# Segment attention with a batch norm: the order of the closing sums, and the split of the output stage over VectorE, TensorE and the queues

## Chip, cores and metric

The kernel runs on one core of one Trainium2 chip. The metric is the device time of one execution in microseconds (us). The kernel before takes 324.0 us, the median of three runs (323.58 to 324.59).

## The reference

16384 rows of 256 floats carry a segment number from 0 to 7 each. The numbers are random and not sorted, yet the start of every segment is looked up with `searchsorted`. Each segment attends over its own rows, the result goes through a matrix, a batch norm over all rows follows, and a relu of it is added to the input.

```python
q, k, v = feat @ Wq, feat @ Wk, feat @ Wv
starts = jnp.searchsorted(bids, jnp.arange(8))
pos = jnp.arange(N) - starts[bids]
qp, kp, vp = pad(q), pad(k), pad(v)            # zeros(8, 3072, .).at[bids, pos].set(.)
attn = softmax(where(mask, qp @ kp.T, -1e9))   # per segment
r = (attn @ vp)[bids, pos]
t = r @ Wt
tn = (t - t.mean(0)) / sqrt(t.var(0) + 1e-5) * gamma + beta
return feat + relu(tn)
```

Because the numbers are not sorted, `pos` can be negative or 3072 and more. A position past an end reads the segment's edge row; a negative one wraps round, and if two rows meet in one place only one of them is stored ("losers" read the other's result). So there are three kinds of output rows: rows that own a place (at most 768 a segment), losers, and rows that read an edge row of some segment.

## The kernel before

`fast_path` writes one instruction stream per engine by hand; a small planner (`Program.op`, `Program.run`) puts in the semaphore waits that the operands call for. Within an engine the order is the order of the code. The helpers record every operation, so many instructions share a line: L803 is every matmul, L813 every activation, L818 and L819 copies on ScalarE and VectorE, L822 `tensor_tensor`, L831 `tensor_scalar`, L842 `scalar_tensor_tensor`, L855 the reciprocal, L878 a gather, L894 a scatter (`put`), L886 a scatter inside a branch (`put_now`).

**Attention.** A loop over the eight segments (`for e in range(NB)`) gathers a segment's rows in tiles of 128 (`xs`), projects, scores, and attends; `attend` leaves the sums and the row weights in PSUM, `scale` writes the rows `tk`, and these are stored in DRAM (`t_rows`). In between, `moments` adds each finished row tile and its square into `acc` on VectorE, and `square` makes the squares on ScalarE.

**The closing sums.** In the last segment, a gather on GpSimd's queue fetches the edge rows into `ecat` from `t_rows`. Edge rows that belong to the last segment are picked out by matmuls into `b_e` and added (L1786), and the square of the sum goes into the other half of `ecat` (L1787). Both lines stand ahead of the last row tile (`u == 3`) in the streams of VectorE and ScalarE. After the loop, two matmuls of 512 columns finish the column sums: `we` times `ecat` (L1876), then `ones` times `acc` (L1877). From `sums` VectorE makes mean, variance, `scale` and `shift`, then the edge rows' outputs `y3` in two bf16 parts (L1878 to L1922).

**The output stage.** The rows of the output are written twice. First every row of 16 *groups* of 1024 rows (1 MB each) is written as input plus edge output; then the owner rows and the losers are scattered over them. A group `k` of eight row tiles is four *pairs* of 512 columns. A one-hot matmul (`hot`, 16 matmuls a group, bf16) puts each row's edge output into PSUM. The list `PAIRS[k]` says how many of the four pairs TensorE adds up itself: `open_group` runs the input through an identity matmul into the same bank, and ScalarE copies the sum back. VectorE adds the other pairs to PSUM (`f` L822).

```python
PAIRS = [1, 1, 0, 0, *(2,) * 7, 1, 1, 0, 1, 0]
```

SyncE's queue then issues the group's `store` (L1960), waits in `finish(stores[k - 1])` (L1953) until the store of the group before has landed and counts it in the semaphore `done`, and may issue a load. There are `NF` = 10 buffers for the 16 groups: groups 0 to 9 are loaded before the stage, groups 10 to 15 within it, one behind the store of each group from 3 to 8 (L1988, L1989). `finish` and the load stand behind the store in one queue, so both wait for what the store waits for.

The order of the groups is a table made from the data, such that groups a segment's rows lie in come early. `upto` holds, for each segment, how many groups have to be done before its rows may be scattered. With the reference's inputs it is 3, 5, 5, 7, 7, 7, 11, 11 for the segments, 11 for the losers. Their row counts are 436, 511, 542, 726, 701, 698, 431 and 468, and there are 199 losers.

`normal(m, 4)` makes the output of a segment's first four row tiles on VectorE, three instructions of 1024 columns; `normal_more` does a fifth and a sixth tile (256 columns) in a branch that is taken only if the segment has them. Before, segment `e` follows group `e + 3`, and the losers (`tl`, three tiles, 768 columns) follow group 11.

On GpSimd, each segment's scatters wait for `done` and for these rows. There are four scatters a segment, seven more in branches that these inputs take (one for segment 2, two each for segments 3, 4 and 5), and `LT` = 3 for the losers, in all 42. Each addresses 128 rows; an index past the end is skipped by the transfer. The scatters count in a semaphore `loose`, and the engine waits at the end until it has the number that the register `rows` holds.

Of the kernel before, what the change touches and what calls it, by code (L numbers as in the profile page):

```python
# [11 lines left out]
I32 = mybir.dt.int32  # L12
BF16 = mybir.dt.bfloat16
F16 = mybir.dt.float16
AF = mybir.ActivationFunctionType
ALU = mybir.AluOpType
# [4 lines left out]
P = 128  # L21
NB = 8
# [6 lines left out]
FT = 6  # L29
FW = FT * P  # L30
LT = 3
# [870 lines left out]
def fast_path(nc, feat, bids, wq, wk, wv, wt, gamma, beta, out, bad):  # L902
    N, D = feat.shape
# [5 lines left out]
    NG = J // GT  # L909
    NL = NB + 1  # L910
    TT = NB * FT
# [14 lines left out]
    def new(name, shape, dtype=F32):  # L926
        nonlocal end
        size = mybir.dt.size(dtype)
        for d in shape[1:]:
            size *= d  # L930
        plan.append((name, shape, dtype, end))
        h = at(name, shape, dtype, end)
        end += size + -size % 32
        return h
# [53 lines left out]
    eidx, ridl, idxo = new("eidx", [P, 1], I32), new("ridl", [P, LT], I32), new("idxo", [P, LT], I32)  # L988
    eps_t = new("eps_t", [P, 1])
    armf, arm = new("armf", [1, NB]), new("arm", [1, NB], I32)  # L990
    upto, order = new("upto", [1, NB + 2], I32), new("order", [1, NG], I32)
    gb = new("gb", [P, 2, 32])
    gt_, bt_ = gb[:, 0, 0:NB], gb[:, 1, 0:NB]
    mq, ss8 = new("mq", [P, 2, NB]), new("ss8", [P, 2, NB])
# [75 lines left out]
    def load(eng, key, ap, hi, lo=0):  # L1070
        def emit(e):
            regs[key] = e.value_load(ap, min_val=lo, max_val=hi)

        pg.op(eng, emit, [ap], [], bare=True)
# [642 lines left out]
    def load_group(k):  # L1717
        f = fb[k % NF]

        def emit(e):  # L1720
            rows = feat[ds(regs[("order", k)] * GR, GR), :]
            return e.dma_start(f[:], rows.rearrange("(p i) d -> p i d", p=P))

        pg.op("SP", emit, [], [f[:]], dma=True)

    for e in range(NB):
        last = e == NB - 1
        n = e + 1
        if e == 1:
            one, two, three_ = edges()  # L1730
            sides = [*side_count(0, below[:]), *side_count(1, above[:])]
            fills = fill_rows()
            work.extend([fills[0], *one, fills[1], two, *sides, fills[2], *three_, lambda: own_of(NB - 1)])
        if not last:
            size_of(n)
        pg.region_of((e,) if last else (e, n))
        if e == 0:
            xt_rest(0)
            values(0, 1)
            project(0, 1)  # L1740
            values(0, 2)
            scores(0, 0, range(4, 6))
            own_of(2)
            zero_fill(2)
        if last:
            for u in (0, 1, 4, 5, 2, 3):
                step(e, u)
                if u == 0:
                    scores(e, 1, range(4))
                    late[2]()  # L1750
                    pg.gather(ecat[:, 0, :], t_rows[0 : (NB - 1) * FW, :], eidx[:], (NB - 1) * FW)
                    for g in range(FIRST, EARLY):
                        load_group(g)
                if u == 1:
                    scores(e, 1, range(4, 6))
                    late[4]()
                if u == 4:
                    late[3]()
                if u == 0:
                    lag[:0] = [(NB, t) for t in range(LT)]  # L1760
                if u == 5:
                    first = square(e, 1)
                    for g in range(EARLY, MID):
                        load_group(g)
                if u == 1:
                    pg.act(row_sum[:], ones[:], AF.Identity, scale=reads_r[:, e * FT + 1 : e * FT + 2])
                if u == 3:
                    any_ = hot[0 : 2 * NB, 0:2, :, :].rearrange("p k u x -> p (k u x)")
                    pg.mm(sums[:], none[0 : 2 * NB, :], any_, start=True, stop=False)
                    by_row(row_sum, first[0], first[2])  # L1770
                if u == 3:
                    while lag or squared:
                        if lag and len(squared) < 2:
                            squared.append(square(*lag.pop(0)))
                        else:
                            moments()
                else:
                    past(e)
                if u == 2:
                    b_e = ps_s[0]  # L1780
                    for u_ in (0, 4, 5, 1):
                        pg.mm(
                            b_e[:, 0:D], sel[:, u_, :], tk[:, e * FT + u_, :], start=(u_ == 0), stop=(u_ == 1),
                            pred=over4(e, u_),
                        )
                    pg.tt(ecat[:, 0, :], ecat[:, 0, :], b_e[:, 0:D], ALU.add)  # L1786
                    pg.act(ecat[:, 1, :], ecat[:, 0, :], AF.Square)  # L1787
        else:
            busy = e + 2 < NB
            step(e, 0, lambda: (xt_main(n, 0), xt_main(n, 1)))  # L1790
            if 0 < e < NB - 3:
                prefix(e + 2, e + 3)
                sizes(e + 2)
            if 0 < e and busy:
                list_ahead(e + 2)
            scores(e, 1, range(4))
            past(e)
            slot()
            if e == NB - 2:
                load_group(0)  # L1800
            step(e, 1)
            xt_rest(n)
            if e == 0:
                prefix(e + 2, e + 3)
                sizes(e + 2)
                list_ahead(e + 2)
            project(n, 0)
            if busy:
                list_part(e + 2, 0)
            scores(e, 1, range(4, 6))  # L1810
            past(e)
            slot(1 if busy else 2)
            step(e, 2, lambda: project(n, 1))
            if busy:
                list_part(e + 2, 1)
            past(e)
            slot(1 if busy else 2)
            if e == NB - 2:
                slot(99)
                load_group(1)  # L1820
                load_group(2)
            if e + 3 < NB:
                zero_fill(e + 3)
            step(e, 3)
            scores(n, 0, range(4))
            if e == NB - 2:
                late[0]()
                late[1]()
            step(e, 4, lambda: values(n, 0))
            past(e)  # L1830
            if e + 4 < NB:
                own_of(e + 3)
            if not busy:
                slot(2)
            if e == 3:
                losers()[0]()
            slot()
            step(e, 5)
            values(n, 1)
            past(e)  # L1840
            if e == 3:
                losers()[1]()
            if e == NB - 4:
                prefix(NB - 1, NB)
                sizes(NB - 1)
                pg.copy("DVE", armf[:], arm[:])
                pg.red(cnt_f[0:1, 0:1], armf[:])
                pg.ts(upto[:, NB + 1 : NB + 2], cnt_f[0:1, 0:1], 16.0, ALU.mult, 16.0 * (4 * NB + LT), ALU.add)
                todo, late = rows()
                work.extend(todo)  # L1850
            scores(n, 0, range(4, 6))
            values(n, 2)
            past(e)
            slot()
        if last:
            assert not lag and not squared
        pg.end_region()
        if e == NB - 2:
            slot(99)
            pg.set("POOL", none[:], 0.0)  # L1860
    for e_ in range(NB + 1):
        load("POOL", ("g", e_), upto[0:1, e_ : e_ + 1], NG, 1)
    for e_ in range(NB):
        load("POOL", ("t", e_), arm[0:1, e_ : e_ + 1], 2)
    load("POOL", "rows", upto[:, NB + 1 : NB + 2], 16 * (TT + LT), 16 * (4 * NB + LT))

    for g in range(MID, NF):
        load_group(g)
# [4 lines left out]
    b_e = ps_s[3]  # L1873
    for x, m in enumerate(last_two):
        pg.mm(b_e[:, 0:D], sel[:, 2 + x, :], tk[:, m, :], start=(x == 0), stop=(x == 1))
    pg.mm(sums[:], we[:], ecat[0 : 2 * NB, :, :].rearrange("p s d -> p (s d)"), start=False, stop=False)  # L1876
    pg.mm(sums[:], ones[:], acc[:].rearrange("p s d -> p (s d)"), start=False, stop=True)  # L1877
    pg.ts(good[:], rdens[:], LIM, ALU.is_lt)  # L1878
    pg.stt(good[:], rdens[:], 1.0 / LIM, good[:], ALU.is_gt, ALU.mult, accum=odd[:])
    pg.ts(odd[:], odd[:], -1.0, ALU.mult, float(TT), ALU.add)  # L1880
# [19 lines left out]
    )  # L1900
    scale, shift = ss[:, 0:D], ss[:, D : 2 * D]

    PAIRS = [1, 1, 0, 0, *(2,) * 7, 1, 1, 0, 1, 0]

    def open_group(k):
        f = fb[k % NF]
# [48 lines left out]
    def store(k, lo, hi):  # L1955
# [5 lines left out]

        return pg.op("SP", emit, [f[:, lo:hi, :]], [], dma=True)

    stores = []
    for k in range(NG):
        f = fb[k % NF]
# [18 lines left out]
        stores.append([store(k, 0, 4), store(k, 4, 8)] if k == 0 else [store(k, 0, 8)])  # L1985
        if k >= 1:
            finish(stores[k - 1])
        if k >= 3 and k - 3 + NF < NG:  # L1988
            load_group(k - 3 + NF)  # L1989
        if 3 <= k < 3 + NB:  # L1990
            e = k - 3
            normal(e * FT, 4)
            normal_more(e, 4)
            normal_more(e, 5)
        if k == 3 + NB:
            normal(0, LT, tl, xl)
    again = {}

    for eng in ENGINES:
# [26 lines left out]
            pg.op("POOL", emit, [idx[:, m : m + 1]], [])  # L2026
    look("POOL")
    pg.op("POOL", lambda x: (x.wait_ge(done, 1), x.wait_ge(done, regs[("g", NB)])), [], [])
    for t in range(LT):
        pg.put(out, idx[:, TT + t : TT + t + 1], tl[:, t, :], N)  # L2030

    held = pg.run("rows")
    held += [done, *row_done]
# [54 lines left out]
```

## Time and profile before

| | us |
|---|---|
| median of three runs | 324.0 |
| the profiled execution's own time | 323.04 |
| its span | 318.4 |
| outside the span | 4.64 |
| VectorE busy over the span | 238.8 |
| TensorE busy over the span | 249.3 |
| GpSimd busy over the span | 133.8 |
| moved in all | 52.49 MB |

Times in the profile count from the span's start. "Idle before" in square brackets names what the trace holds to be the last wait that ended; a wait for several semaphores is put down to one of them. The share of DMA is the mean busy share of the 16 DMA engines; it can read slightly over 1. The clock column is TensorE's granted clock, 1.00 or 0.50 and means of these.

### The profile page before, as it was taken

How to read it: one execution, taken by the hardware profiler on the slowest of the kernel's cores; microseconds unless marked ns; L12 is line 12 of the kernel's file. 1: busy time of each engine (PE TensorE's matmuls, PEld its weight loads, DVE VectorE, ACT ScalarE, POOL GpSimd, SP SyncE). 2: the span in 40 equal slices, each digit the busy share in tenths (PEclk: the TensorE clock that was granted, in tenths of full speed). 3: DMA queues.
4: the chain of work that ended last, by engine and by line, in shares of the span. 5: the costliest groups of instructions: out<-in, count | busy, mean ns of one | idle time of the engine just before them, and what ended most of it. 6: DMA issues, size and time to landing. Idle time of an engine off the chain costs nothing.

```text
span 318.4 us, 4632 instructions
## 1 busy us (share of the span) xinstructions
PE 249.3 (78%) x1279; PEld 162.2 (51%) x1279; DVE 238.8 (75%) x773; ACT 150.3 (47%) x294; POOL 133.8 (42%) x143
## 2 busy tenths in 40 slices
PE   4699779998999999989999999859776955642600
PEld 2465547675676777667766777547322322210200
DVE  4845759988669576748776889866679999999930
ACT  3126949884764485255736557749501221111000
POOL 7433307051071034223502463776040337787873
PEclk9559979999999999999999999997965897775555
DMA  3101104114047014210300135198997999998795
GB/s 104 35 23 28 40 2 129 52 54 141 6 87 169 1 29 126 97 31 19 106 33 3 33 104 165 20 333 342 337 402 300 372 398 418 415 414 342 311 374 199
DMA packets 21533, 52.49 MB, mean 165 GB/s; under 512 B 5488, under 2 KB 14786, under 8 KB 17530
## 3 DMA queue, kind: packets, MB, share of 16 engines
q1 hardware_dynamic: 15674, 41.37, 34.6%
q0 software_dynamic: 5280, 10.18, 11.0%
q10 hardware_dynamic: 544, 0.52, 0.5%
q8 instruction: 15, 0.25, 0.3%
q14 instruction: 20, 0.16, 0.2%
HBM read 26.27 MB, written 28.74 MB: 173 GB/s over the span
## 4 chain that ended last, share of the span: by engine, by line
PE 41%; DVE 26%; ACT 11%; issue 9%; POOL 6%; DMA 4%; another core or an unknown queue 1%; POOLq 1%; DVEq 0%; SPq 0%
PE ps L803 39%; DVE tk L822 6%; DVE f L822 5%; POOL out L894 4%; ACT pa L813 4%; ACT xT L813 2%; PE ps L808 2%; DMA ecat<-t_rows,eidx 2%; ACT vs L818 2%; DMA t_rows<-tk 2%; DVE junk L829 2%; DVE k L819 1%; DVE tk L1942 1%; DVE tk L1944 1%; ACT xs L818 1%
## 5 line engine op out<-in xcount | busy, mean ns | idle before, releaser
L878 POOL DMA_INDIRECT xs<-in_r_feat,idx x48 | 50.8, 1059 | 100.3 <-DVE idx L842 52.0
L803 PE MATMUL ps<-vs,pa 128*128 128x257 f32 x312 | 78.0, 394 | 7.2 <-ACT vs L818 3.8
L803 PEld LDWEIGHTS ps<-vs,pa 128*128 128x128 f32 x312 | 57.9, 194 | 20.7 <-issue 7.5
L894 POOL DMA_INDIRECT out<-tk,idx x32 | 34.4, 1075 | 28.4 <-DVE tk L842 19.2
L803 PE MATMUL ps<-wvt,xT 128*128 128x256 f32 x156 | 37.5, 386 | 1.5 <-ACT vs L818 0.7
L818 ACT COPY f<-ps 128x1024 f32<-128x1024 f32 (+1 forms) x12 | 9.8, 835 | 58.7 <-PE ps L803 56.1
L803 PE MATMUL ps<-y,hot 32*128 32x256 bf16 x256 | 14.3, 353 | 26.5 <-DVE f L822 16.8
L803 PEld LDWEIGHTS ps<-wvt,xT 128*128 128x128 f32 x156 | 28.8, 190 | 11.3 <-ACT sq L813 2.3
L813 ACT ACTIVATE pa<-ps,mask 128x512 f32<-128x512 f32 x48 | 29.5, 687 | 10.6 <-PE ps L803 9.3
L803 PE MATMUL ps<-f,ident 128*128 128x512 f32 x38 | 29.0, 893 | 1.7 <-DVE f L822 1.2
L803 PEld LDWEIGHTS ps<-y,hot 32*128 32x128 bf16 x256 | 6.5, 111 | 43.6 <-DVE f L822 25.2
L822 DVE TENSOR_TENSOR f<-f,ps 128x1024 f32<-128x1024 f32 (+3 forms) x17 | 26.0, 1559 | 3.5 <-remote 2.9
L819 DVE COPY k<-ps 32x128 f32<-32x128 f32 x48 | 14.1, 294 | 17.5 <-PE ps L803 16.7
L818 ACT COPY vs<-ps 128x512 f32<-128x512 f32 x24 | 14.2, 590 | 25.2 <-PE ps L803 16.6
L813 ACT ACTIVATE q<-ps,cqk 96x512 f32<-96x512 f32 (+3 forms) x32 | 18.4, 573 | 13.6 <-PE ps L803 13.2
L855 DVE RECIPROCAL rdens<-ps 128x1 f32<-128x1 f32 x48 | 7.7, 160 | 22.6 <-PE ps L803 22.6
L803 PE MATMUL ps<-xT,w 128*128 128x512 f32 (+1 forms) x48 | 22.4, 593 | 2.3 <-ACT xT L813 2.3
L813 ACT ACTIVATE xT<-ps,negx 128x512 f32<-128x512 f32 (+1 forms) x32 | 17.0, 586 | 15.2 <-PE ps L808 9.8
L842 DVE SCALAR_TENSOR_TENSOR acc<-tk,reads_r,acc 128x256 f32<-128x256 f32 x45 | 21.4, 477 | 1.5 <-issue 1.3
L842 DVE SCALAR_TENSOR_TENSOR acc<-sq,reads_r,acc 128x256 f32<-128x256 f32 x45 | 21.5, 477 | 0.3 <-ACT sq L813 0.3
L878 POOL DMA_INDIRECT reads_r<-reads_of,idx x12 | 12.0, 1003 | 23.0 <-DVE ge L831 11.7
L813 ACT ACTIVATE pb<-ps,mask 128x256 f32<-128x256 f32 x48 | 19.3, 483 | 4.0 <-PE ps L803 3.8
(271 smaller groups left out, 426.2 us busy)
## 6 DMA issues: line engine op xcount, KB each, us to landing
f<-in_r_feat SPq DMA_DIRECT2D x16, 1024.0 KB, 7.7
out<-f SPq DMA_DIRECT2D x15, 1024.0 KB
t_rows<-tk SPq DMA_DIRECT2D x8, 512.0 KB, 4.2
t_rows<-tk SPq DMA_DIRECT2D x8, 256.0 KB, 2.2
eb<-edge_of SPq DMA_DIRECT2D x16, 64.0 KB
out<-f SPq DMA_DIRECT2D x2, 512.0 KB, 2.7
xs<-in_r_feat,idx POOLq DMA_INDIRECT x48, 3.6
out<-tk,idx POOLq DMA_INDIRECT x39
```

The lines of the kernel that those rows point to most:

```text
L803: "PE", lambda e: e.matmul(out, lhsT, rhs, start=start, stop=stop, skip_group_check=True),
L808: return self.op("PE", lambda e: e.transpose(out, in_, ident), [in_, ident], [out], pred=pred)
L813: "ACT", lambda e: e.activation(out, in_, func, bias=bias, scale=scale), [in_, *more], [out]
L818: return self.op("ACT", lambda e: e.copy(out, in_), [in_], [out])
L819: return self.op(eng, lambda e: e.tensor_copy(out, in_), [in_], [out])
L822: return self.op(eng, lambda e: e.tensor_tensor(out, a, b, op), [a, b], [out])
L829: lambda e: e.tensor_scalar(out, a, s1, s2, op0, op1, accum_out=accum)
L842: else e.scalar_tensor_tensor(out, a, s, b, op0, op1),
L855: return self.op("DVE", lambda e: e.reciprocal(out, in_), [in_], [out])
L878: lambda e: e.indirect_dma_start(out=out, out_offset=None, in_=table, in_offset=bass.IndirectOffsetOnAxis(ap=ind, axis=0), bounds_check=n ...
L894: lambda e: e.indirect_dma_start(out=table, out_offset=bass.IndirectOffsetOnAxis(ap=ind, axis=0), in_=src, in_offset=None, bounds_check=n ...
L1942: v.tensor_tensor(y, y, scale, ALU.mult).then_inc(sem, 1)
```

## The change

1. **Sums.** The add of `b_e` into `ecat` and its square move from ahead of the last row tile to behind all `moments`. The two closing matmuls change places: `acc` first, `ecat` last.
2. **Empty tile.** A register `lost` tells whether there are more than 256 losers. The third tile's scatter stands in a branch on it, and `rows` counts it only then. Two VectorE instructions on one element and one register load on GpSimd are new.
3. **Order of the segments' rows.** Segment 0 follows group 2, segments 1 to 5 follow groups 4 to 8, segments 6 and 7 groups 10 and 11, the losers group 12.
4. **Loads.** Groups 10 to 15 are loaded behind the stores of groups 4 to 9.
5. **Pairs.** By the two lists, TensorE and ScalarE have 29 of the 64 pairs instead of 19, VectorE 35 instead of 45.

```diff
-                    pg.tt(ecat[:, 0, :], ecat[:, 0, :], b_e[:, 0:D], ALU.add)
-                    pg.act(ecat[:, 1, :], ecat[:, 0, :], AF.Square)
...
-                pg.ts(upto[:, NB + 1 : NB + 2], cnt_f[0:1, 0:1], 16.0, ALU.mult, 16.0 * (4 * NB + LT), ALU.add)
+                lost = n_bc[0:1, NB : NB + 1]
+                pg.ts(upto[:, NB + 2 : NB + 3], lost, (LT - 1.0) * P, ALU.is_gt)
+                pg.stt(cnt_f[0:1, 0:1], lost, (LT - 1.0) * P, cnt_f[0:1, 0:1], ALU.is_gt, ALU.add)
+                pg.ts(upto[:, NB + 1 : NB + 2], cnt_f[0:1, 0:1], 16.0, ALU.mult, 16.0 * (4 * NB + LT - 1), ALU.add)
...
         if last:
             assert not lag and not squared
+            pg.tt(ecat[:, 0, :], ecat[:, 0, :], b_e[:, 0:D], ALU.add)
+            pg.act(ecat[:, 1, :], ecat[:, 0, :], AF.Square)
...
+    load("POOL", "lost", upto[:, NB + 2 : NB + 3], 1)
...
-    pg.mm(sums[:], we[:], ecat[0 : 2 * NB, :, :].rearrange("p s d -> p (s d)"), start=False, stop=False)
-    pg.mm(sums[:], ones[:], acc[:].rearrange("p s d -> p (s d)"), start=False, stop=True)
+    pg.mm(sums[:], ones[:], acc[:].rearrange("p s d -> p (s d)"), start=False, stop=False)
+    pg.mm(sums[:], we[:], ecat[0 : 2 * NB, :, :].rearrange("p s d -> p (s d)"), start=False, stop=True)
...
-    PAIRS = [1, 1, 0, 0, *(2,) * 7, 1, 1, 0, 1, 0]
+    PAIRS = [1, 1, 0, 2, 1, *(3,) * 5, *(2,) * 3, 1, 1, 1]
...
+    AFTER = {2: (0,), 4: (1,), 5: (2,), 6: (3,), 7: (4,), 8: (5,), 10: (6,), 11: (7,), 12: (NB,)}
...
-        if k >= 3 and k - 3 + NF < NG:
-            load_group(k - 3 + NF)
-        if 3 <= k < 3 + NB:
-            e = k - 3
-            normal(e * FT, 4)
-            normal_more(e, 4)
-            normal_more(e, 5)
-        if k == 3 + NB:
-            normal(0, LT, tl, xl)
+        if k >= 4 and k - 4 + NF < NG:
+            load_group(k - 4 + NF)
+        for e in AFTER.get(k, ()):
+            if e < NB:
+                normal(e * FT, 4)
+                normal_more(e, 4)
+                normal_more(e, 5)
+            else:
+                normal(0, LT, tl, xl)
...
-    for t in range(LT):
+    for t in range(LT - 1):
         pg.put(out, idx[:, TT + t : TT + t + 1], tl[:, t, :], N)
+
+    def put_last(x):
+        with x.If(regs["lost"] > 0):
+            pg.put_now(x, out, idx[:, TT + LT - 1 : TT + LT], tl[:, LT - 1, :], N)
+
+    pg.op("POOL", put_last, [idx[:, TT + LT - 1 : TT + LT], tl[:, LT - 1, :]], [])
```

More of the change, by code (lines that the diff above doesn't have):

```diff
@@ L990, in fast_path @@
     armf, arm = new("armf", [1, NB]), new("arm", [1, NB], I32)
-    upto, order = new("upto", [1, NB + 2], I32), new("order", [1, NG], I32)
+    upto, order = new("upto", [1, NB + 3], I32), new("order", [1, NG], I32)
     gb = new("gb", [P, 2, 32])
@@ L1864, in fast_path @@
         load("POOL", ("t", e_), arm[0:1, e_ : e_ + 1], 2)
-    load("POOL", "rows", upto[:, NB + 1 : NB + 2], 16 * (TT + LT), 16 * (4 * NB + LT))
+    load("POOL", "rows", upto[:, NB + 1 : NB + 2], 16 * (TT + LT), 16 * (4 * NB + LT - 1))
+    load("POOL", "lost", upto[:, NB + 2 : NB + 3], 1)
     for g in range(MID, NF):
```

## The prediction

> **What bounds the kernel now.** I read the page's slices first, to see where the kernel changes its kind of work.
>
> ```profile
> DVE  4845759988669576748776889866679999999930
> ...
> PEclk9559979999999999999999999997965897775555
> DMA  3101104114047014210300135198997999998795
> ```
>
> One digit is 8 us. From slice 30 (239 us) VectorE (DVE) is full and so are the DMA engines: that is the output stage, where all but the first edit lie. The first lies just ahead, so I took the timeline of 215 to 240, by engine.
>
> ```profile
> 226.66 0.42 DVE L822 TENSOR_TENSOR ecat<-ecat,ps 128x256 f32<-128x256 f32 x1 [1.95 <-DMA ecat<-t_rows,eidx]
> 227.00 0.16 DVE L855 RECIPROCAL rdens<-ps 128x1 f32<-128x1 f32 x1
> ...
> 231.91 0.72 DVE L858 STREAM_TRANSPOSE st_t<-ps 128x512 f32<-128x512 f32 x1 [1.78 <-PE ps L803]
> ...
> 227.44 0.46 ACT L813 ACTIVATE tk<-ps,rdens 128x256 f32<-128x256 f32 x1
> ...
> 228.58 1.29 PE L803 MATMUL ps<-ecat,we 16*128 16x512 f32 x2
> 229.80 2.07 PE L803 MATMUL ps<-acc,ones 128*128 128x512 f32 x2
> ```
>
> VectorE waits for the gathered edge rows, and the last tile's reciprocal, which does not need them, queues behind. So ScalarE's last rows, the last sums and both closing matmuls come late, and nothing else runs.
>
> Then the output stage. GpSimd's timeline shows where its scatters (one instruction each) run without a rest:
>
> ```profile
> 260.88 1.07 POOL L894 DMA_INDIRECT out<-tk,idx  x1 [4.34 <-DVE tk L842]
> ...
> 313.10 0.98 POOL L894 DMA_INDIRECT out<-tl,idx  x1 [0.30 <-issue]
> ```
>
> SyncE's queue shows when groups go out (`out<-f`) and are loaded (`f<-in_r_feat`):
>
> ```profile
> 251.97 0.34 SPq L1960 DMA_DIRECT2D out<-f  x1
> 253.56 0.30 SPq L1722 DMA_DIRECT2D f<-in_r_feat  x1
> 256.79 0.34 SPq L1960 DMA_DIRECT2D out<-f  x1
> 260.24 0.36 SPq L1722 DMA_DIRECT2D f<-in_r_feat  x1
> ```
>
> A table of windows shows how full the DMA is (columns: length; busy time of TensorE, its weight loads, VectorE, ScalarE and GpSimd; clock, share of the DMA engines, GB/s):
>
> ```profile
> 240.00:242.00 2.00, 1.37 (x16) 0.55 (x16) 2.00 (x3) 0.28 (x1) 0.00 (x0) 0.50 0.33 129
> 242.00:288.00 46.00, 29.73 (x178) 10.59 (x176) 45.04 (x51) 7.57 (x8) 25.56 (x23) 0.76 1.01 405
> 288.00:302.00 14.00, 5.42 (x58) 2.09 (x62) 13.76 (x12) 0.80 (x2) 10.95 (x11) 0.50 0.78 310
> 302.00:313.00 11.00, 0.74 (x16) 0.21 (x8) 3.59 (x2) 0.37 (x1) 8.35 (x9) 0.50 1.01 382
> 313.00:317.00 4.00, 0.00 (x0) 0.00 (x0) 0.00 (x0) 0.00 (x0) 0.98 (x1) 0.50 0.41 145
> ```
>
> GpSimd never rests from 260.88 to 314.08: 38 scatters in 53.2 us, 1.40 each. The wait at 260.88 is put down to VectorE, but segment 1's rows were done at 255.5; what came just before is the load at 260.24, which stands behind `finish(4)` in SyncE's queue. Segment 1 needs five groups done, so this is `done` = 5: group 4, issued at 251.97, took 8 us to land with two loads of 1 MB round it. The chain of waits names VectorE up to 290 and the scatters after that; but the windows say that the DMA engines are a second bound of nearly the same length.
>
> I count them in full time: 0.66 + 46.5 + 10.9 + 11.1 + 1.6 = 70.8 of share, at a full 1.01 that is 70.1 us from 240.0 to the last landing near 317.2. The rest, 7.1 us, is idle: 1.4 at the start, 3.2 in 288 to 302, 2.4 at the end. No edit changes what groups are stored and loaded or which rows are scattered, so 70.1 stays.
>
> **Sums (part 1).** Freed, the reciprocal runs when VectorE is through at 224.7; ScalarE is through with its square at 225.2, makes the last rows by 225.7 and the square by 226.2. Six moments of 0.40 run 224.8 to 227.2. Then `ecat` (landed at 226.66, not later by anything here) is added until 227.6 and squared until about 228.1. TensorE starts `acc` 0.3 after the last moment (before: 229.53 to 229.80), at 227.5. At the clock of that row (0.50) it ends at 229.6, then `ecat` takes 1.3: the transpose of `sums` starts at 230.9, 1.0 earlier. At a full clock (two passes of 0.5, as the identity matmuls of the same width take at 1.00: 1.98 for four passes) it ends at 228.5 and `ecat` at 229.5: 2.4 earlier. The clock stood at 1.00 until 229.4, so I take 2.0. It carries on: from the transpose to the first group (231.91 to 239.15) VectorE is one chain, and the loads and the row store that ScalarE's last rows release (227.92 to 230.4) go out 2 us earlier too.
>
> **Empty tile (2).** 199 losers are under 256, so the branch is not taken: one scatter, 1.3 to 1.4 us, off GpSimd's chain, nothing off the DMA's, as its indices are all past the end. The two element-wide instructions (0.15 to 0.2 each by such rows) stand in segment 4, where TensorE is full: 0, or 0.3 if nothing covers them. The register load runs while GpSimd waits 12.0 us for `t_rows`.
>
> **Pairs (5).** VectorE's `f` rows: 1.21 for 1024 columns, 1.75 for 1536, 2.28 for 2048, so 0.54 a pair; ten fewer save 5.4 of its 69.3 us. The cost goes to TensorE, 1.0 a pair at clock 1.00 and 1.9 to 2.0 at 0.50 (four passes took 3.75 to 4.05), and to ScalarE, 1.44 for three pairs by its rows of 0.59 and 1.01. ScalarE is idle. TensorE in groups 5 to 9 needs three pairs and the one-hot 16: 3.6 us at 1.00, 6.9 at 0.50. VectorE's cycle there is 0.6 for the add and 6.24 for a segment of six tiles, 6.84. So at 0.50 TensorE just fails to keep up. The windows show a clock of 0.76 in this stretch, and a full 3.4 us of work (246.5 to 249.9) followed by 1.00. By the mean clock a group takes 3.6 / 0.76 = 4.7, which the 6.84 hide; if that cover is gone, the third rival has the price. I cost it at 0.
>
> The Trainium skill, "TensorE: Matmul & The Clock Gate", "Why this matters for your kernels", wants no TensorE gaps over about 3 us, else half the clock. That speaks against the change: a warm group (3.6 of 6.84) leaves such a gap. The trace agrees so far that the clock fell to 0.50 four times between 263 and 284, with gaps of 3 to 4 us. By the rule alone every group would start cold: 3.4 us at half speed, then 1.9, an estimate of 5.3 a group, still under 6.84.
>
> **Order and loads (3, 4).** With 2.0 taken off, group 2's add ends at 242.8, then segment 0's rows take 3.65 and group 3's two pairs 1.13: group 3 goes out at 247.8 instead of 247.2. Segment 0 needs `done` = 3, which is counted behind that store, so its scatters start near 249. The DMA runs dry meanwhile: group 2's data, issued at 242.9, is through about 3.7 after its issue (before, group 2 landed at 249.5, issued at 244.86), and group 3's starts 0.6 after its own: a new hole of 1.7, at least 1.0, at most 2.1. The first load now comes behind group 4's store, so group 4 goes out at 249.5 and lands by 254.5, behind 1 MB and four scatters only. Group 5's store is issued at 253.8, segment 1's rows are done at 253.0, so `done` = 5 and the second run of scatters come at 255.0, 5.9 earlier. With 37 scatters of 1.40 GpSimd would end at 306.8, and land 3.1 later, as before (314.08 to 317.2): 309.9. The loads themselves come some 2 us later (group 10's near 252, before 249.78), which delays nobody: it is needed near 280.
>
> **The sum.** Of the two bounds the DMA is now the later. Its work starts at 238.0; 70.1 of work, 1.4 at the start, 1.7 of new hole. The 3.2 between 288 and 302 came from VectorE handing over groups slower than the DMA took them; with 5.4 less to do it falls behind no more, I leave 0.7. The last 2.4, scatters alone and skew, I leave. 238.0 + 70.1 + 1.4 + 1.7 + 0.7 + 2.4 = 314.3, against 317.2: 2.9 less. That is 320.1 on this execution's 323.04, which lies 0.96 under the median; on the median of 324.0 it is 321.1. Ends: shift 2.4, hole 1.0, middle 0, tail 1.4 give 311.5, or 318.3 on the median; shift 1.0, hole 2.1, middle 2.2, tail 2.4 give 317.2, or 324.0.
>
> **Rivals.**
> *Scatters set the end, not the DMA* (8%). If transfers overlap better than their shares say, 309.9 stands: 7.3 less, 316.7. Against it, 1.01 for 46 us.
> *Only the start moves* (13%). If `acc` runs cold (1.0), the hole is 2.1 and 1.5 to 2.5 of the middle idle stay, the time is 323.3 to 324.3. The later loads speak for it: the DMA has less queued early.
> *TensorE at half clock* (13%, slower). It sits in `open_group` from group 5 on: five groups of 6.9, three of 4.95, three of 3.0, 58.4 us. From 249.0 that is 307.4, and the last one-hot sums were seen 3.7 late (matmuls at 302.3, VectorE's add at 306.16), so the last add, 1.75 long, ends at 312.9. A store needs 5 to 8 us to land (308.48 to about 316.3): 318 to 321, 1 to 4 later, 325.0 to 327.8. It decides once a pair takes over 1.83 us on the mean: 249.0, 24 pairs, 11 one-hot groups of 1.0, then 3.7, 1.75 and 5 make the 314.3 of the sum. For it: 0.50 throughout from 284. Against: the windows in which work of one full 3.4 us brought 1.00.
> *The branch is taken or the order table differs*: the inputs exclude it.
>
> **Numbers.** 321.1 has 66%. The first rival is faster too: faster 0.74, same 0.13, slower 0.13, with a bound of 0.3% (1.0 us), about what a measurement here can tell from none. The range runs from 317.5, a part of the way to the first rival, to 325.0, the near end of the third.
>
> **What would show it.** Right: no wait ahead of the last reciprocal, `acc` ahead of `ecat` and the transpose 1.0 to 2.4 earlier; 41 scatters, the second run from about 255; the DMA full from 249 to past 300 with a hole near 247; the last scatter's issue some us ahead of the end. Wrong: TensorE's busy time filling the stage at 0.50 with VectorE's `f` waiting on it; or scatters waiting at `done` = 7 or 11 until they set the end again; or the hole spreading into the groups after it.

## The result and the profile after

| | before | after |
|---|---|---|
| median of 11 runs, us | 323.58 (322.53 to 324.59) | 321.86 (319.38 to 322.65) |
| profiled execution, us | 323.04 | 322.49 |
| its span, us | 318.4 | 317.8 |
| last reciprocal of `rdens` / transpose of `sums` | 227.00 / 231.91 | 227.60 / 232.39 |
| first group's add | 239.15 | 239.72 |
| last landing / end, counted from that add | 78.0 / 79.3 | 76.9 / 78.1 |

The ratio of the runs is 0.9927, with a 95% interval of 0.9900 to 0.9953: the kernel became 2.4 us faster, by 1.5 to 3.2 (the medians differ by 1.7). The time fell into the likeliest case, 0.8 over the number predicted. The runs of after lie in two clumps, five at 319.4 to 320.5 and six at 321.9 to 322.6; the profiled one is of the upper clump, so its 0.6 us against the profile of before is less than the change is worth.

The page's slices first (a digit is 7.9 us):

```profile
DVE  4845659988676866847867889872979999999620
PEclk9559979999999999999999999995975999788555
DMA  3101103214035005310310134099799899999994
```

Counted from 0, the notch that DMA had in slices 36 and 37 (8 and 7) is gone: it is full through slice 38. Granted clock is up in slices 31, 33, 35 and 36, and VectorE thins out from slice 37 on. The windows of the output stage, with the columns that the prediction explains:

```profile
240.00:246.00 6.00, 4.32 (x27) 1.72 (x20) 6.00 (x5) 0.89 (x2) 0.00 (x0) 0.50 0.90 358
246.00:248.00 2.00, 2.00 (x20) 0.62 (x18) 1.93 (x3) 0.42 (x1) 0.00 (x0) 0.86 0.97 406
248.00:250.00 2.00, 1.05 (x18) 0.33 (x16) 2.00 (x2) 1.18 (x2) 0.00 (x0) 1.00 0.78 315
250.00:252.00 2.00, 1.67 (x4) 0.87 (x5) 2.00 (x3) 0.00 (x0) 0.35 (x1) 1.00 0.50 197
...
250.00:288.00 38.00, 27.55 (x172) 10.83 (x172) 37.11 (x49) 9.22 (x7) 24.38 (x23) 0.91 0.98 386
288.00:302.00 14.00, 6.94 (x52) 2.33 (x52) 11.02 (x10) 2.19 (x3) 11.14 (x10) 0.60 1.00 409
302.00:312.00 10.00, 0.00 (x0) 0.00 (x0) 1.75 (x1) 0.59 (x1) 7.56 (x9) 0.50 0.99 387
312.00:314.00 2.00, 0.00 (x0) 0.00 (x0) 0.00 (x0) 0.00 (x0) 0.57 (x1) 0.50 0.69 256
```

The DMA's share from 288 to 302 went from 0.78 to 1.00: 3.1 us of idle are gone. In their place stands the new hole, 0.78 and 0.50 from 248 to 252: 2 x 0.23 + 2 x 0.50 = 1.5 us. The clock from 250 to 288 is 0.91; before it was 0.81 in the same stretch (from 242 on it was 0.76, now 0.88).

The sums, from the timeline by engine:

```profile
227.60 0.16 DVE L855 RECIPROCAL rdens<-ps 128x1 f32<-128x1 f32 x1
...
230.05 0.41 DVE L822 TENSOR_TENSOR ecat<-ecat,ps 128x256 f32<-128x256 f32 x1
...
232.39 0.72 DVE L858 STREAM_TRANSPOSE st_t<-ps 128x512 f32<-128x512 f32 x1 [1.33 <-PE ps L803]
```

No wait stands in front of the last reciprocal or of `ecat`. From the reciprocal before the last to the transpose it is now 5.64 us, before 8.13. Still the transpose comes 0.48 later than before, because the last segment itself began later: its first reciprocal is at 218.26, before at 215.72. That is in code the change doesn't touch. Counted to the transpose from the last `acc<-tl` (VectorE adds the last tile of the losers' rows to `acc`), the sums took 9.78 before and take 7.29 now. Before:

```profile
222.13 0.48 DVE L842 SCALAR_TENSOR_TENSOR acc<-tl,ones,acc 128x256 f32<-128x256 f32 x1
```

After:

```profile
225.10 0.48 DVE L842 SCALAR_TENSOR_TENSOR acc<-tl,ones,acc 128x256 f32<-128x256 f32 x1
```

GpSimd's scatters after the start of each run, from its timeline (the others of 41 follow 0.30 after one another):

```profile
251.65 1.03 POOL L894 DMA_INDIRECT out<-tk,idx  x1 [12.68 <-SPq L1957]
...
258.43 0.98 POOL L894 DMA_INDIRECT out<-tk,idx  x1 [1.86 <-SPq L1957]
...
274.35 1.19 POOL L894 DMA_INDIRECT out<-tk,idx  x1 [3.83 <-SPq L1957]
...
311.58 0.99 POOL L894 DMA_INDIRECT out<-tl,idx  x1 [0.30 <-issue]
```

All three waits are now put down to SyncE's queue (`finish`): `done` = 3, 5 and 7. The last one is new. And the last groups on VectorE:

```profile
297.70 1.75 DVE L822 TENSOR_TENSOR f<-f,ps 128x1536 f32<-128x1536 f32 x1 [0.20 <-remote]
306.35 1.75 DVE L822 TENSOR_TENSOR f<-f,ps 128x1536 f32<-128x1536 f32 x1 [6.90 <-remote]
```

TensorE's matmuls for that last add are recorded at 297.8 to 298.8. Their semaphore comes at 306.26.

### The profile page after: what moved, and what is told of

It is laid out like the page before. It is cut to its first block, busy times and chain, and to the rows that moved or that the text cites. A ratio compares the mean times of both kernels' runs of the same rounds, so it can differ in the third digit from the quotient of the medians.

```text
span 317.8 us, 4687 instructions
## 1 busy us (share of the span) xinstructions
PE 253.8 (80%) x1299; PEld 164.8 (52%) x1299; DVE 233.9 (74%) x775; ACT 156.0 (49%) x297; POOL 131.9 (42%) x142
## 4 chain that ended last, share of the span: by engine, by line
PE 44%; DVE 25%; ACT 11%; issue 9%; POOL 6%; another core or an unknown queue 3%; DVEq 0%; POOLq 0%
PE ps L803 42%; DVE tk L822 6%; DVE f L822 4%; ACT pa L813 4%; POOL out L894 4%; ACT xT L813 2%; PE ps L808 2%; ACT vs L818 2%; DVE acc L842 2%; DVE junk L829 1%; DVE k L819 1%; DVE tk L1946 1%; DVE tk L1948 1%; ACT xs L818 1%
## 5 line engine op out<-in xcount | busy, mean ns | idle before, releaser
L803 PE MATMUL ps<-vs,pa 128*128 128x257 f32 x312 | 79.2, 398 | 8.6 <-ACT vs L818 8.4
L894 POOL DMA_INDIRECT out<-tk,idx x32 | 33.5, 1046 | 27.2 <-SPq L1957 18.4
L818 ACT COPY f<-ps 128x512 f32<-128x512 f32 (+2 forms) x15 | 14.7, 984 | 59.4 <-PE ps L803 32.8
L803 PE MATMUL ps<-f,ident 128*128 128x512 f32 x58 | 35.5, 741 | 7.0 <-issue 4.9
L822 DVE TENSOR_TENSOR f<-f,ps 128x512 f32<-128x512 f32 (+3 forms) x17 | 20.8, 1245 | 7.7 <-remote 7.1
L813 ACT ACTIVATE q<-ps,cqk 96x512 f32<-96x512 f32 (+3 forms) x32 | 18.4, 574 | 13.6 <-PE ps L803 13.3
L803 PE MATMUL ps<-y,hot 32*128 32x256 bf16 x256 | 12.4, 308 | 12.4 <-DVE f L822 7.3
L803 PEld LDWEIGHTS ps<-f,ident 128*128 128x128 f32 x58 | 11.4, 220 | 19.7 <-issue 18.7
```

Source lines behind the costliest of these rows:

```text
L803: "PE", lambda e: e.matmul(out, lhsT, rhs, start=start, stop=stop, skip_group_check=True),
L813: "ACT", lambda e: e.activation(out, in_, func, bias=bias, scale=scale), [in_, *more], [out]
L818: return self.op("ACT", lambda e: e.copy(out, in_), [in_], [out])
L822: return self.op(eng, lambda e: e.tensor_tensor(out, a, b, op), [a, b], [out])
L894: lambda e: e.indirect_dma_start(out=table, out_offset=bass.IndirectOffsetOnAxis(ap=ind, axis=0), in_=src, in_offset=None, bounds_check=n ...
```

## Experiments

Theory: the DMA sets the end of the output stage, so that every us in which it idles there is a us of time. Rivals: GpSimd's chain of scatters, which from `done` = 7 on runs without a rest to 312.57; and the last groups on VectorE and TensorE, which come as late as ever. The kernels ran in three sets, each on a chip of its own with the kernel before beside it. Changes in us are worked out as (ratio - 1) x that set's median of before, 321.79, 323.65 and 321.78.

What each profile shows, read from windows of it as length minus share / 1.01 for the DMA's idle, with times counted from the first group's add (the first column: from the last reciprocal but one to the transpose of `sums`):

| kernel | sums | DMA idle 8 to 17 | DMA idle 50 to 64 | last add | last scatter ends | last landing |
|---|---|---|---|---|---|---|
| before | 8.13 | 0.1 | 3.1 | 67.0 | 74.9 | 78.0 |
| after | 5.64 | 1.5 | 0.1 | 66.6 | 72.8 | 76.9 |
| part 1 alone (e1) | 8.22 | 1.9 | 2.3 | 64.4 | 76.5 | 79.2 |
| all but part 1 (e2) | 9.31 | 1.6 | 0.3 | 59.4 | 72.9 | 76.7 |
| part 5 alone (e3) | 7.71 | 0.8 | 0.9 | 62.4 | 74.5 | 77.3 |
| all but part 5 (e5) | 5.81 | 1.6 | 0.1 | 64.1 | 73.3 | 78.0 |
| after again (e8) | 7.05 | 1.5 | 0.1 | 59.3 | 72.8 | 76.5 |
| all but part 1 again (e12) | 6.91 | 1.5 | 0.2 | 59.3 | 72.8 | 76.8 |
| all but part 5 again (e15) | 7.09 | 2.5 | 0.0 | 64.1 | 74.0 | 78.2 |
| segment 0 behind group 3 (e13) | 6.90 | 3.2 | 0.4 | 62.0 | 74.1 | 78.5 |
| no losers' scatters (e9) | 5.65 | 1.2 | 0.2 | 65.1 | 70.2 | 76.3 |

The table leaves out the first 8 us after the add, in which loads that were issued before the stage still run. There the DMA idles between 0.5 us (e5) and 2.1 (e1), and from the add on it has between 28.1 and 29.1 MB to move. So the two columns of idle do not give the last landing by themselves: e5 has the idle of after but 0.5 MB more to move, and lands 1.1 later. A profile is also one execution only; it lies between 1.8 under the median of its kernel (e5) and 2.7 over it (e3).

**First set: the parts one by one.** Part 1 alone, on the kernel before:

```diff
-                    pg.tt(ecat[:, 0, :], ecat[:, 0, :], b_e[:, 0:D], ALU.add)
-                    pg.act(ecat[:, 1, :], ecat[:, 0, :], AF.Square)
...
+            pg.tt(ecat[:, 0, :], ecat[:, 0, :], b_e[:, 0:D], ALU.add)
+            pg.act(ecat[:, 1, :], ecat[:, 0, :], AF.Square)
...
-    pg.mm(sums[:], we[:], ecat[0 : 2 * NB, :, :].rearrange("p s d -> p (s d)"), start=False, stop=False)
-    pg.mm(sums[:], ones[:], acc[:].rearrange("p s d -> p (s d)"), start=False, stop=True)
+    pg.mm(sums[:], ones[:], acc[:].rearrange("p s d -> p (s d)"), start=False, stop=False)
+    pg.mm(sums[:], we[:], ecat[0 : 2 * NB, :, :].rearrange("p s d -> p (s d)"), start=False, stop=True)
```

> The kernel before with part 1 alone (the edge rows last in the sums). Theory: the shift of the sums carries through to the end one for one, 2.0 us less (1.0 to 2.5), near 321.6; in the trace no wait ahead of the last reciprocal and `acc` ahead of `ecat`. Rival: the output stage takes the shift back, since the DMA engines are still busy with the loads before it and set the end: 0 to 0.7 less.

Measured: 1.0003 (0.9976 to 1.0030), +0.1 us (-0.8 to +1.0). Alone it brings no gain that can be measured, against the 2.0 of the prediction; why is seen in the third set.

The changed kernel without that same edit (e2):

> The changed kernel without part 1 (the old order of the sums; new order of the rows, loads, pairs, empty tile). Theory: the output stage alone gives 0.9 us (0.4 to 1.5), so near 322.7. Rival: the output stage gives all of the gain and the sums none, about 2.4 less, near 321.2.

Measured: 0.9973 (0.9944 to 1.0002), -0.9 us (-1.8 to +0.1): parts 2 to 5 together have the size of the 0.9 that the prediction's sum gave the stage.

The new list of pairs alone, on the kernel before (e3):

```diff
-    PAIRS = [1, 1, 0, 0, *(2,) * 7, 1, 1, 0, 1, 0]
+    PAIRS = [1, 1, 0, 2, 1, *(3,) * 5, *(2,) * 3, 1, 1, 1]
```

> The kernel before with the new list of pairs alone. Theory: VectorE's 5.4 us less bring 0 to 1.0, because the DMA engines and the scatters set the end; the DMA's idle time between 288 and 302 shrinks. Rival: VectorE sets the pace, 4 to 5 us less. Rival: TensorE at half clock, 1 us more or worse.

Measured: 0.9957 (0.9929 to 0.9985), -1.4 us (-2.3 to -0.5): the one part that shows a gain by itself in this set.

The changed kernel with the old list (e5, the diff above backwards):

> The changed kernel with the old list of pairs. Theory: the pairs are worth 0 to 1.0, so this is 1.4 to 2.4 under the kernel before. Rival: the new order of rows and loads lives from the shorter VectorE work; without it the last groups come later than the scatters and the time is that of the kernel before or more.

Measured: 0.9979 (0.9945 to 1.0013), -0.7 us (-1.8 to +0.4), too near the others to rank it by time. The table shows the odd thing: the idle from 50 to 64 goes from 3.1 to 0.9 with the pairs alone, and to 0.1 without them, by the order and the later loads alone. In e1, whose output stage is that of before, it is 2.3, so a column of this table moves by 0.8 from profile to profile. The gains of the parts overlap and do not add.

**Second set: what sets the end.** The changed kernel without the loads of groups 10 to 15 (e4):

```diff
-        if k >= 4 and k - 4 + NF < NG:
-            load_group(k - 4 + NF)
```

> The changed kernel without the six loads of groups 10 to 15 (6 x 1 MB; those groups then add to whatever their buffers held, so the output of their rows is not the reference's). DMA sets the end of the output stage: at the 390 to 400 GB/s of the full windows 6 MB are 15.5 us of DMA work, so far more than VectorE can follow; the end then falls to the next bound, the scatters (28 without a rest from the wait for the seventh group's landing) and that wait itself comes earlier since group 6's store has no loads beside it: 3 to 5 us less than the changed kernel, about 317. Scatter chain alone sets the end: it starts when the seventh group has landed; without loads beside it that is 3 us earlier at most, and 28 scatters of 1.37 follow: 1 to 3 less. VectorE or TensorE set the end (last group's sums late at 306): 0 to 1 less.

Measured: 1.0095 (1.0050 to 1.0139), +3.1 us. Nobody expected it slower. From the timelines of VectorE and TensorE:

```profile
279.17 0.68 DVE L822 TENSOR_TENSOR f<-f,ps 128x512 f32<-128x512 f32 x1
295.92 1.22 DVE L822 TENSOR_TENSOR f<-f,ps 128x1024 f32<-128x1024 f32 x1 [16.06 <-remote]
```

```profile
283.99 0.51 PE L803 MATMUL ps<-y,hot 32*128 32x256 bf16 x12
285.29 0.26 PE L803 MATMUL ps<-y,hot 32*128 32x256 bf16 x1 [0.79 <-issue]
286.00 0.26 PE L803 MATMUL ps<-y,hot 32*128 32x256 bf16 x1 [0.45 <-issue]
287.42 0.36 PE L803 MATMUL ps<-y,hot 32*128 32x256 bf16 x1 [1.15 <-issue]
288.82 0.36 PE L803 MATMUL ps<-y,hot 32*128 32x256 bf16 x1 [1.03 <-issue]
```

Sixteen one-hot matmuls take 0.6 to 1.0 us elsewhere. Here the last ones start 0.71 to 1.42 apart, waiting for nothing that the profile shows, and VectorE gets the sums 7 us after the last of them. Meanwhile it stands for 16 us. So TensorE set the end of this run by its profile, and it tells nothing about the DMA.

One load put into the hole (e7, group 10's behind group 2's store):

```diff
-        if k >= 4 and k - 4 + NF < NG:
+        if k == 2:
+            load_group(NF)
+        if k >= 5 and k - 4 + NF < NG:
```

> The changed kernel with group 10's load two stores earlier (behind group 2's store instead of group 4's), so that 1 MB (2.6 us of DMA work) is queued across the hole of 1.5 us near 249. If the DMA sets the end, that hole closes: 1.0 to 1.5 less than the changed kernel. If the chain of scatters from the seventh group's landing sets the end: the bytes ahead of that store are the same, 0 to 0.5 less. Against it: group 3's landing, which releases the first scatters, comes up to 2.6 later; if that is what counts, 0 to 1 more.

Measured: 1.0167 (1.0108 to 1.0226), +5.4 us. The hole did shrink (0.8 of idle instead of 1.5), but VectorE stood 7.2 and 13.3 us for TensorE in the same manner:

```profile
300.63 1.03 PE L803 MATMUL ps<-y,hot 32*128 32x256 bf16 x13
302.37 0.37 PE L803 MATMUL ps<-y,hot 32*128 32x256 bf16 x1 [0.71 <-issue]
303.76 0.37 PE L803 MATMUL ps<-y,hot 32*128 32x256 bf16 x1 [1.01 <-issue]
```

```profile
314.40 3.42 DVE L822 TENSOR_TENSOR f<-f,ps 128x1536 f32<-128x1536 f32 x2 [13.33 <-remote]
```

What the load does by itself stays open, since it was run on this chip only.

The empty tile's scatter put back (e6: `LT` for `LT - 1` in both counts and in the loop of puts, the branch left out):

> The changed kernel with the empty tile's scatter put back (part 2 undone): one GpSimd scatter of 1.37 more, no DMA bytes more. If the DMA sets the end: 0 to 0.3 more than the changed kernel. If the chain of scatters sets the end: 1.3 to 1.4 more. If VectorE's last group does: 0 to 0.5 more.

Measured: 0.9887 (0.9828 to 0.9946), -3.7 us. It is not slower than the changed kernel (0.9927), but VectorE waited 11.68 for its last sums in its profile, so the end was not the scatters' to set, and it does not separate the theories.

The losers' last two scatters left out (e9: the loop of puts and the branch removed, the count to match):

> The changed kernel without the losers' last two scatters (199 rows of 1 KB, so those rows are not written as the reference has them). Two scatters of 1.37 less on GpSimd, 0.2 MB or 0.5 us less for the DMA. If the chain of scatters sets the end: 2.5 to 2.7 less than the changed kernel. If the DMA sets it: 0.5 to 0.7 less. If VectorE's last group sets it, whose store lands near the same time: 0 to 1 less.

Measured: 0.9917 (0.9884 to 0.9951), against 0.9927 for the changed kernel in the first result: 0.3 less, not 2.5. The profile is plainer than the time. Its last scatter:

```profile
309.99 0.98 POOL L894 DMA_INDIRECT out<-tk,idx  x1 [0.30 <-issue]
```

GpSimd ends at 70.2 instead of 72.8, that is 2.6 earlier, as two scatters would give; the last landing is at 76.3 instead of 76.9, 0.6 earlier, as their bytes would give. The chain of scatters does not set the end. The last store of VectorE's groups could (TensorE kept it waiting 5.76 here, 6.90 in after); that rival falls with e8 below.

**Third set: the changed kernel again, with one part undone at a time.** This chip did not show TensorE's standing. The changed kernel itself (e8):

> The changed kernel itself, once more, beside the three that follow. It should be 1.0 to 2.5 us below the kernel before. If TensorE stands late in the output stage again, as in its first profile (last sums 8 us after their matmuls), the end of the stage still comes 77 to 79 us after the first group's add; the last add may move by 7 us without moving the end, if the DMA sets it.

Measured: 0.9931 (0.9904 to 0.9957), -2.2 us; median 319.73. From its timeline of VectorE and its windows:

```profile
292.35 5.07 DVE L822 TENSOR_TENSOR f<-f,ps 128x1536 f32<-128x1536 f32 x3
```

```profile
288.00:302.00 14.00, 3.43 (x34) 1.08 (x34) 9.25 (x8) 1.17 (x2) 10.75 (x11) 0.62 1.00 405
302.00:312.00 10.00, 0.00 (x0) 0.00 (x0) 0.00 (x0) 0.00 (x0) 5.62 (x6) 0.50 0.81 316
```

The last store in SyncE's queue:

```profile
305.57 0.33 SPq L1964 DMA_DIRECT2D out<-f  x1
```

The last three adds follow each other without a wait, and VectorE is through 59.3 + 1.7 after the first add, 7.3 earlier than in the first profile of the same kernel. The last landing is at 76.5 instead of 76.9. So seven us of VectorE and TensorE are worth 0.4 at the end, as long as the DMA is full: the last store is not issued at 61 but at 69.2, behind the `finish` of the stores before it.

Part 1 undone (e12, the same kernel as e2):

> The changed kernel without part 1 (the sums in the old order). If the sums are worth what the prediction says: 1.0 to 2.4 us more than the changed kernel. By the profiles so far (from the fifth reciprocal to the transpose of the sums 5.6 to 5.8 in the five runs of kernels with all the rest and part 1, 7.7 to 9.3 without it): 2 to 3.5 more. If the wait for the gathers takes its place, as in the run of part 1 alone: 0 to 0.5 more.

Measured: 0.9943 (0.9910 to 0.9976), -1.8 us; median 319.89, 0.16 over e8. Part 1 is worth 0.2 to 0.4 us here; by the means of the runs it is 0.6, with an interval of -0.2 to 1.3. VectorE and the closing matmuls in e8, then in e12:

```profile
219.96 0.51 DVE L842 SCALAR_TENSOR_TENSOR acc<-tl,ones,acc 128x256 f32<-128x256 f32 x1 [0.17 <-DMA tl<-t_rows,ridl]
...
223.88 0.17 DVE L855 RECIPROCAL rdens<-ps 128x1 f32<-128x1 f32 x1 [1.27 <-PE ps L803]
...
228.72 0.72 DVE L858 STREAM_TRANSPOSE st_t<-ps 128x512 f32<-128x512 f32 x1 [1.33 <-PE ps L803]
...
226.50 1.12 PE L803 MATMUL ps<-acc,ones 128*128 128x512 f32 x2 [0.42 <-DVE acc L842]
227.56 1.12 PE L803 MATMUL ps<-ecat,we 16*128 16x512 f32 x2
```

```profile
221.24 0.48 DVE L842 SCALAR_TENSOR_TENSOR acc<-tl,ones,acc 128x256 f32<-128x256 f32 x1
...
225.82 0.42 DVE L822 TENSOR_TENSOR ecat<-ecat,ps 128x256 f32<-128x256 f32 x1 [1.84 <-DMA ecat<-t_rows,eidx]
226.16 0.16 DVE L855 RECIPROCAL rdens<-ps 128x1 f32<-128x1 f32 x1
...
229.96 0.72 DVE L858 STREAM_TRANSPOSE st_t<-ps 128x512 f32<-128x512 f32 x1 [0.67 <-PE ps L803]
...
227.74 1.12 PE L803 MATMUL ps<-ecat,we 16*128 16x512 f32 x2
228.79 1.13 PE L803 MATMUL ps<-acc,ones 128*128 128x512 f32 x2
```

From `acc<-tl` to the transpose it is 8.76 with part 1 and 8.72 without. With part 1 the reciprocal no longer stands behind the add's wait of 1.84 for the gather, but waits 1.27 for TensorE, whose clock was down when it made that tile's sums (0.63 in this window of e8):

```profile
219.00:222.00 3.00, 2.71 (x7) 2.17 (x8) 2.66 (x14) 2.90 (x9) 1.90 (x3) 0.63 1.02 426
```

And behind the last of the `moments` (in e8 done at 225.97 + 0.48) both matmuls now stand in a row, where in the old order `ecat` was multiplied from 227.74, before the last of them was done (228.68 in e12). The new order puts that one matmul behind them, about 1.06.

Part 5 undone (e15, the same kernel as e5):

> The changed kernel with the old pairs on TensorE (part 5 undone). If the DMA sets the end and VectorE has some us to spare: 0 to 1 more than the changed kernel. If VectorE sets it: 3 to 5 more. If TensorE, late with the last groups, sets the end: 1 to 4 less than the changed kernel.

Measured: 0.9947 (0.9909 to 0.9984), -1.7 us; median 320.99, 1.3 over e8. By the means of the runs it is only 0.3 (-0.9 to +1.5), so the time does not tell the two apart. Without its two pairs on TensorE, group 3's add is one of 2048 columns and its store goes out 1.0 later; the hole is 2.5 instead of 1.5. But in e5, the same kernel with the same late store, it is 1.6, and e15 idles 0.5 less than e8 in the first 8 us. The 1.7 by which the last landing is later are therefore not explained by the hole alone; 0.3 MB more had to be moved from the add on. VectorE's last add comes 4.8 later, which the last landing does not follow.

Segment 0 behind group 3 (e13):

```diff
-    AFTER = {2: (0,), 4: (1,), 5: (2,), 6: (3,), 7: (4,), 8: (5,), 10: (6,), 11: (7,), 12: (NB,)}
+    AFTER = {3: (0,), 4: (1,), 5: (2,), 6: (3,), 7: (4,), 8: (5,), 10: (6,), 11: (7,), 12: (NB,)}
```

> The changed kernel with the first segment's rows scaled behind group 3, as before, and all else as in the changed kernel. Group 3's store goes out 3.6 us earlier, and the hole of 1.5 us in the DMA near 249 is filled; the first scatters need those rows and start at most 0.5 later. If the DMA sets the end: 1.0 to 1.5 less than the changed kernel. If the scatters do, from the wait for the fifth or seventh group's landing on: those landings come 0 to 1.5 earlier, 0 to 1 less. If VectorE or TensorE does: 0.

Measured: 0.9988 (0.9959 to 1.0017), -0.4 us; median 321.84, 2.1 over e8. I expected the hole to close, and it doubled. VectorE's group 3 and the windows of e13, then the windows of e8:

```profile
244.69 1.22 DVE L822 TENSOR_TENSOR f<-f,ps 128x1024 f32<-128x1024 f32 x1 [2.60 <-PE ps L803]
```

```profile
246.00:248.00 2.00, 2.00 (x13) 0.93 (x6) 1.97 (x2) 0.58 (x1) 0.00 (x0) 1.00 0.70 283
248.00:250.00 2.00, 1.51 (x19) 0.45 (x17) 1.97 (x3) 0.36 (x1) 0.00 (x0) 1.00 0.67 266
250.00:252.00 2.00, 0.62 (x2) 0.41 (x3) 2.00 (x2) 1.08 (x1) 1.18 (x2) 1.00 0.03 12
```

```profile
246.00:248.00 2.00, 1.03 (x3) 0.58 (x4) 2.00 (x2) 0.59 (x1) 0.00 (x0) 1.00 0.25 86
248.00:250.00 2.00, 2.00 (x17) 0.75 (x19) 1.97 (x3) 0.00 (x0) 1.42 (x2) 1.00 0.94 385
250.00:252.00 2.00, 2.00 (x17) 0.91 (x9) 1.97 (x2) 1.44 (x1) 1.60 (x2) 1.00 1.08 438
```

Right behind group 2, group 3's pairs are not done: VectorE waits 2.60 for TensorE, which runs at half clock there (0.50 from 236 to 244). In the changed kernel segment 0's rows fill that wait. Here they come afterwards, group 4 goes out at 251.36 instead of 248.61, and the DMA idles 3.2 instead of 1.5. The 1.7 more of idle become 2.0 at the last landing and 2.1 in the median (1.9 by the means, 1.1 to 2.7). What the DMA loses is what the time shows. VectorE's last add moved by 2.7 and GpSimd's last scatter by 1.3, which fit the 2.0 less well.

## Why the prediction was right, step by step

**The bound.** That the DMA, not the scatters, would be the later bound held: e9 took 2.6 off the scatters and 0.6 off the end, e8 took 7.3 off VectorE's last add and 0.4 off the end, and the hole in e13 passed nearly one to one into the time. The first rival (scatters set the end) is out. GpSimd itself was mis-sized: its last scatter ended 72.8 after the first add, where 306.8 minus the predicted add of 237.15 is 69.7. The 70.1 us of DMA work that was to stay is 70.0 to 73.2 from the first add on in the profiles of the table, as more or less of the earlier loads runs over into the stage. GpSimd's missing 3.1 are a wait of 3.83 at `done` = 7, which the text named as a way to be wrong but left out of the sum; it cost nothing, for the DMA was busy.

**New hole.** 1.7 predicted, 1.5 measured in after, and 1.5 or 1.6 in e2, e5, e8 and e12 (1.2 in e9, 2.5 in e15).

**The middle idle.** 3.2 to 0.7 predicted, 3.1 to 0.1 measured. But the step that was to do it, 5.4 us less on VectorE, was not needed for it. VectorE did get 5.3 us shorter (its `f` rows sum to 26.5 before and 21.2 after). With the old pairs the idle is gone as well (e5, e15), while in e3, with the new pairs and the old order, 0.9 is left. So the pairs close most of it alone, and the order and the loads one group later close it without them. In after the last load goes out 45.6 after the first add instead of 39.9, so the DMA has work queued there; the order and the loads were not undone separately, so which of the two does it is not shown. I had written of the later loads that they delay nobody, and gave them no credit.

**Sums.** Where it could be tested, this term was mis-sized: 2.0, with 1.0 at least, was predicted; e8 against e12 shows 0.2 to 0.6, and e1 shows 0.1 the wrong way, a gain of 0.8 at most. The wait for the gather went, as said. But I let the last reciprocal run as soon as VectorE was free, at 224.7 in before's profile. Its other input, TensorE's output, was there in time in that profile (the matmuls end at 224.18). In e8 the reciprocal still waits for it until 223.88, 1.6 ahead of the gather's landing (225.43), and in e1 until 225.83, 0.2 behind it (225.58). In these two TensorE had stood 1.9 and 3.9 us just ahead of the last tile, and its clock was at 0.50 afterwards. And the second matmul that now comes last takes back about 1.06.

In the profiles of after, e4, e6, e7 and e9 TensorE stood earlier in the segment, its clock was back at 1.00 for the last tile, and no wait is left: from `acc<-tl` to the transpose they all take 7.3, against 9.78 before. That is 2.5 less, about what was predicted. Part 1 alone, or the rest without it, never ran beside these, so how much of the result's 2.4 is part 1 stays open.

**Empty tile.** Costed at nothing on the DMA's path. The experiment for it (e6) was overlaid by TensorE; e9, with two scatters less, supports it.

**TensorE at half clock.** The third rival did not come: the clock from 250 to 288 was 0.91, up from 0.81, and TensorE's ten pairs more (25.0 us of identity matmuls from 239 on before, 31.8 after) hid behind VectorE, as costed. Over all profiles it is 0.81 to 0.91 in this stretch with the new pairs, 0.68 to 0.81 with the old. The estimate that the Trainium skill's rule gave ("TensorE: Matmul & The Clock Gate", "Why this matters for your kernels": gaps of over about 3 us halve the clock), every group cold at 5.3, was too high: with three pairs a group TensorE works groups ahead and rarely has a gap that long. In after the clock stood at 1.00 from 246.6 to 273.9, over a gap of 2.2 us, and fell to 0.50 in one of 4.2, which agrees with the rule. VectorE did wait for TensorE at the end (6.90), but from another cause than the clock, and e8, without that wait, ends 0.4 earlier.

**The sum.** 2.9 predicted: 2.0 from the sums and 0.9 from the stage. Measured 2.4 and 2.2, of it 1.1 at the last landing in the first pair of profiles. Without part 1 it is -1.8 (-2.9 to -0.8) in e12, so in the third set the stage gave most of it: there, by these figures, the total was right with one term too large and one too small, which is luck. In e2, the same kernel on another chip, it is -0.9 (-1.8 to +0.1), which fits the predicted 0.9. For the result itself the split is not shown. None of the variants is measurably faster than the changed kernel.

## What to carry to other kernels

When the DMA is full to the end of a stage, look for its idle and price an edit by the idle that it opens or closes; us saved on an engine that hands work to a full queue are worth little (seven us of VectorE: 0.4). Moving loads later may also keep the DMA fed where the producer is slow (here it was moved together with the order), and work put between two stores can cost one hole and close another. And when one input of an instruction is made early, ask for its second-latest input before writing down a gain.

## What I had not expected of the hardware

TensorE stood late in the output stage in some runs and not in others, whatever the kernel. In the profiles of before, after and the second set, above all from about 263 on, many of its semaphores come late, up to 12.3 us after the end of the last recorded one-hot matmul of a group (e6), and one-hot matmuls that start 0.04 to 0.07 us apart elsewhere start 0.7 or 1.4 apart in e4 and e7. In the first and third set, on other chips, the semaphores follow that end within 0.1 us. The same traces that show it hold about 2,940 to 3,040 semaphore events, the others 4,270 to 4,300. The kernel before is slower there too, 323.58 and 323.65 against 321.79 and 321.78. Whether that is the chip, or the recording of the profile holding TensorE back, was not settled. It can set the end: nothing else that the profiles of e4 and e7 show makes them slower than the kernel before. Why it costs these two kernels 3 to 5 us, and e6 and e9, whose last adds wait 11.68 and 5.76 on the same chip, no time that can be seen, is open.

TensorE also stands 2 to 5 us somewhere between 209 and 218 in the profiles of before, after and the second set; in the others it stands 1.9 to 4.1 us between 216 and 223, waiting for ScalarE (`pb`). With all but identical code up to there, the first group's add came at 234.4 to 240.8 in e4, e6, e7, e9 and after. A single profile is therefore no measure for a term of one or two us ahead of the output stage, and counting from a mark inside the stage is what made the stage's own terms readable.
